# A preactivated convolution: sums and differences gathered in one PSUM bank, and two thirds of the images combined

## The chip, the cores and the metric

The kernel runs on one core of a Trainium2 chip. The metric is device time in microseconds, the median of the runs. The engines are named as in the profile: PE is TensorE, PEld its weight loads, DVE is VectorE, ACT is ScalarE, POOL is GpSimd, SP is SyncE, which here issues DMAs only.

## The reference

The input `x` is 160 images of 128 channels and 32 x 32 pixels. Each is normalised over groups of 4 channels, convolved 3 x 3 (padding 1) with one of 5 weight sets (image b*5+n in the reshaped batch uses set n), and added to `x`. The weights are quantised first, by two nested floors.

```python
    # weights: w = s1*floor(U/s1) + s2*floor((U - v1)/s2), s1 = (max U - min U)/3, s2 = s1/5
    w = (v1 + v2).reshape(OUT_CH * N, IN_CH, K, K)
    xb = x.reshape(B // N, N * C, H, W)
    act = conv_general_dilated(xb, w, window_strides=(1, 1), padding=[(1, 1), (1, 1)], feature_group_count=N)
    ...
    # _gn: 32 groups of 4 channels, over channels and pixels
    ((g - m) / jnp.sqrt(s + 1e-5)).reshape(v.shape)
    ...
    x = x + _L0_conv_ref(_gn(x), L0_conv_U)
```

## The kernel before

**Tiling.** One image is one step: 128 channels on the partitions, 1024 pixels along them. The kernel's own index i runs over the images of one weight set after the other, 32 per set. Images come in chunks of two (`load`, L492) and go out twice: `store_input` writes the input itself to the output, and `accumulate` (L949) later adds the convolution to it in DRAM with an accumulating DMA issued by GpSimd. Only the first three and the last four images (`by_hand`) are added by VectorE.

**Fewer multiplications.** Two neighbouring outputs of a 3-tap filter (g0, g1, g2) are made of four products instead of six: with inputs d0 to d3, the products are (d0-d2)g0, (d1+d2)(g0+g1+g2)/2, (d2-d1)(g0-g1+g2)/2 and (d1-d3)g2. Even is the sum of the first three, odd is the second minus the third minus the fourth. In the code the four are quarters 0, 2, 3 and 1 of a tile of 2048 columns. The weights of quarters 2 and 3 are called SUM and DIFF and are made by `both_sums` (L571).

**Two kinds of images.** Values are in float16, as a high part and a low part (what rounding left over).

- A *combined* image (`combined`, L651) takes the four combinations of neighbouring columns in float32 (`combine` on VectorE, L684; `beside_pairs` on GpSimd, L701), then the high part vh (`high_combined`, ScalarE, L735) and the low part vl (`low_combined`, VectorE, L741). Both go through four quarters of three matmuls: 24 matmuls.
- An image that is *not combined* is normalised to z (GpSimd, or ScalarE for some), its high part goes through all nine taps for each parity of rows (`taps`, L775: 18 matmuls), and only its low part through the four quarters (`combinations`, L758: 12 matmuls): 30 matmuls.

From image 7 to 29 every second image is combined, from 30 to 129 three of five, then three of four.

**One round.** The loop in `run` (L983) goes over i. TensorE does in `conv(i)` (L862): the quarters 3 and 2 of image i+1, as `sums_of_pairs` (L854), into the banks m2 and m1a or m1b; then `main(i, 0)` and `main(i, 1)` (L878), which add quarters 0 and 1 (and the taps) on top of the even and the odd bank of image i. In the same round ScalarE copies half of m2 to SBUF (`leave`, L888), and VectorE writes both banks of image i+1 with two instructions:

```python
        nc.vector.scalar_tensor_tensor(even, m1, 0.5, m2, ALU.mult, ALU.add)
        between()
        nc.vector.scalar_tensor_tensor(odd, m1, 0.5, m2, ALU.mult, ALU.subtract)
```

The PSUM holds two pairs of banks (`eo`, four banks), m1a, m1b, m2 and one bank for small things. The finished pair of banks of image i-1 is copied to SBUF by ScalarE (`residual`, L921, one copy of 1024 columns) for the accumulating DMA.

**Order.** It is written out by hand: each engine runs its instructions in the order of the code. In a round ScalarE does the first measurement pass of an image some 15 ahead, `residual(i-1)`, `leave(i+1)`, a high part, the second measurement pass. VectorE does a low part with its combinations, steps of the next weight set's quantisation (`later`), `pairs(i+1)`, `combine`, and, for a few images (`BY_VECTOR`), the whole measurement. `step_of` (L973) tells which image a step is for; from round 11 on the three preparing steps run one image further ahead than before, so that rounds 11 to 13 each hold one step more.

Of the kernel before, what the change touches and what calls it, by code (L numbers as in the profile page):

```python
# [25 lines left out]

LIFT = 2.0**14
LEAST, MOST = 2.0**-10, 0.04
# [357 lines left out]
class Main:  # L386
# [41 lines left out]
    def __init__(self, tc, ctx, keep, x, u, out):  # L428
        self.tc = tc
        nc = self.nc = tc.nc  # L430
        self.imgs, C, self.H, self.W = x.shape
        P = self.P = nc.NUM_PARTITIONS
        assert C == P and self.H * self.W == 1024
        self.per_set = self.imgs // N_SETS
        self.xv = x.rearrange("(b n) c h w -> n c b (h w)", n=N_SETS)
        self.ov = out.rearrange("(b n) c h w -> n c b (h w)", n=N_SETS)
        self.uv = u.rearrange("n (o i k) -> n o i k", o=C, k=TAPS)

        def pool(name, bufs, **kw):
# [12 lines left out]
        self.evac = pool("evac", 2)  # L452
        self.sums = pool("sums", 3)
        self.unread = pool("unread", 1)
        self.small = pool("small", 3)
        self.ps_eo = pool("ps_eo", 2, space=PSUM)
        ps_m = pool("ps_m", 1, space=PSUM)
        ps_small = pool("ps_small", 1, space=PSUM)
        self.steps = Steps(nc, keep)

        self.m1a, self.m1b, self.m2_ps = (
            ps_m.tile([P, self.H // 2, self.W], F32, tag=name, name=name)
            for name in ("m1a", "m1b", "m2")
        )
        self.pair = [self.m1a, self.m2_ps]
# [3 lines left out]
        self.chunks, self.z, self.hi, self.v, self.eo, self.m2 = {}, {}, {}, {}, {}, {}  # L469
        self.sum, self.stored = {}, {}  # L470
        self.tables, self.wts, self.across = {}, {}, {}
        self.columns = []
# [48 lines left out]
    def over_partitions(self, ext1, ident, between):  # L521
# [3 lines left out]

        place = self.bank_pair("range").rearrange("p h r w -> p h (r w)")
        rows = place[0:1, 0, : 2 * P].rearrange("p (k c) -> p k c", k=2)
        for k in range(2):
# [3 lines left out]
        nc.vector.tensor_reduce(top, rows, AX.X, ALU.max)  # L532
        spread = place[:, 1, :2]
        nc.tensor.matmul(spread, self.ones, top, start=True, stop=True)
# [71 lines left out]
    def by_vector(self, i):  # L606
        return i in self.BY_VECTOR

# [42 lines left out]
    def combined(self, i):  # L651
# [123 lines left out]
    def taps(self, i, part, col, target, parities=(0, 1)):  # L775
# [7 lines left out]
        for k in self.KS:  # L783
            for a in parities:
# [3 lines left out]
                nc.tensor.matmul(  # L788
                    self.bank(target, a)[:, first:end, c0:c1],
                    self.wts[n, col][:, k, :],  # L790
# [5 lines left out]

    def bank_pair(self, i):
        return self.ps_eo.tile([self.P, 2, self.H // 2, self.W], F32, tag="eo", name=f"eo{i}")

    def bank(self, target, h):  # L800
        return target[h] if isinstance(target, list) else target[:, h]

    def warm_up(self, count):


        zeros = self.los[3].rearrange("p h w -> p (h w)")
        for _ in range(count):
            self.nc.tensor.matmul(
                self.pair[0].rearrange("p i w -> p (i w)"), zeros[:, :128],
                zeros[:, :512], start=True, stop=True,  # L810
            )

    def direct_hi(self, i, col):

        if i not in self.eo:
            self.eo[i] = self.bank_pair(i) if i < 2 else self.pair
        self.taps(i, (self.hi[i], 0), col, self.eo[i])
# [28 lines left out]

    def m1(self, i):
        return self.m1b if i % 2 else self.m1a
# [12 lines left out]

    def conv(self, i, on_the_way):  # L862


        if self.FIRST < i < self.imgs - 1:
            self.sums_of_pairs(i + 1)
        if i == self.FIRST:
            self.main(i, 0)
            self.sums_of_pairs(i + 1)
            on_the_way(self.COLS[1])  # L870
            self.main(i, 1)
            on_the_way(self.COLS[2])
        else:
            self.main(i, 0, lambda: on_the_way(self.COLS[1]))
            self.main(i, 1, lambda: on_the_way(self.COLS[2]))
        del self.v[i]

    def main(self, i, a, between=lambda: None):  # L878

        to = self.bank(self.eo[i], a)  # L880
        for step in self.KS:
# [6 lines left out]
    def leave(self, i):  # L888

        m2 = self.evac.tile([self.P, self.H // 2, self.W], F32, tag="m2", name=f"m2_{i}")  # L890
        self.nc.scalar.mul(m2, self.m2_ps, 0.5)  # L891
        self.m2[i] = m2

    def pairs(self, i, between=lambda: None):


        nc = self.nc
        m1, m2 = self.m1(i), self.m2.pop(i)
        eo = self.eo[i] = self.bank_pair(i)
        if i == self.imgs - 1:  # L900
            eo = self.eo[i] = [eo[:, 0], self.m1(i - 1)]
        even, odd = (self.bank(eo, a) for a in range(2))
        nc.vector.scalar_tensor_tensor(even, m1, 0.5, m2, ALU.mult, ALU.add)
        between()
        nc.vector.scalar_tensor_tensor(odd, m1, 0.5, m2, ALU.mult, ALU.subtract)  # L905

# [5 lines left out]

    def flat(self, i, banks):
        return banks.rearrange("p a i w -> p a (i w)") if self.combined(i) else banks

# [5 lines left out]
    def residual(self, i):  # L921
# [19 lines left out]
        image = self.as_banks(i, xj)  # L941
        if eo is self.pair:
            for a in range(2):
                nc.vector.tensor_add(image[:, a], self.bank(eo, a), image[:, a])
        else:
            nc.vector.tensor_add(image, self.flat(i, eo), image)
        self.store(i)
# [35 lines left out]
    def run(self):  # L983
# [42 lines left out]
        for i in range(2):  # L1026
            self.measure(i)
        first_means = self.bank_pair("means").rearrange("p h r w -> p h (r w)")
        spread = self.over_partitions(
            ext1, ident, lambda: self.stats_of(0).means(first_means[:, 0])  # L1030
        )
# [32 lines left out]
        measure(1, 3)  # L1064
        self.stats[1].means(first_means[:, 1])
        self.stats[1].deviations()
# [48 lines left out]
        for i in range(self.imgs):  # L1115
# [15 lines left out]
            if i < self.FIRST:  # L1131
                if i == self.FIRST - 1:
                    self.sums_of_pairs(self.FIRST)

                j = (i - 1) % self.FIRST
                self.direct_hi(j, self.COLS[2])
                self.direct_lo(j, self.COLS[2])
                if i == 0:
                    self.stats[2].variances()
# [26 lines left out]
            if i < self.FIRST:  # L1166
# [6 lines left out]
                if i == 2:  # L1173
                    self.leave(3)
                    self.normalise(5)
                    measure(1, 9)
                    self.high_part(5)
                    self.pairs(3)
                    self.low_part(4)
# [3 lines left out]
            else:  # L1183
# [132 lines left out]
```

## Time and profile before

| | |
|---|---|
| median of 3 runs | 966.45 us (965.62 to 966.77) |
| profiled execution | 964.56 us, span 962.5 us |
| granted TensorE clock | 0.995 |
| PE busy | 927.8 us (96%), 4432 matmuls |
| DVE busy | 902.6 us (94%) |
| ACT busy | 862.7 us (90%) |
| POOL busy | 460.1 us (48%) |
| DMA | 254.22 MB, mean 264 GB/s |

The page gives the busy time of each engine, its share in 40 slices of the span, and groups of instructions with the number, the mean duration, and what ended the idle time before them. In its names, `m` is m2 (the PSUM bank and its copy alike, since numbers are left out), `eo` the pairs of banks, `vh` and `vl` the high and low parts of a combined image, `hi`, `lo` and `rows` those of the others. A matmul's duration (0.37 us) holds a part that overlaps the next one; the distance from start to start (0.21 us) is what it takes of TensorE.

### The profile page before, as it was taken

What the parts mean: (1) busy time and instruction counts of PE and PEld (TensorE: products, weight loads), DVE (VectorE), ACT (ScalarE), POOL (GpSimd) and SP (SyncE); (2) the same over time, 40 slices, a digit from 0 to 9 for tenths busy, and PEclk for the clock granted to TensorE, in tenths of its full rate; (3) what the DMA queues carried; (4) which work ended last, traced back from release to release, by engine and by line L of the source; (5) the groups of instructions that cost most, each with busy time, mean ns of one, the idle gap of its engine ahead of it and who ended that gap; (6) DMA issues with size and microseconds to landing.
All of it is one profiled execution on the core that took longest, in us unless ns stands there. A gap on an engine that the chain in (4) does not pass through costs nothing.

```text
span 962.5 us, 13034 instructions
## 1 busy us (share of the span) xinstructions
PE 927.8 (96%) x4432; PEld 433.8 (45%) x4432; DVE 902.6 (94%) x1269; ACT 862.7 (90%) x1167; POOL 460.1 (48%) x477
## 2 busy tenths in 40 slices
PE   2899989999999999999999999999999999999997
PEld 1344434444444444444444444444444444444443
DVE  7989999999899999989999999899999998999993
ACT  5879989999899999999999999999999999997660
POOL 4344434456445445554545445545444366565640
PEclk9999999999999999999999999999999999999999
DMA  9079999999999999999999999999999999856563
GB/s 349 36 267 345 334 348 320 325 321 325 328 321 323 317 295 308 272 306 254 295 251 289 284 293 297 282 277 286 267 273 267 282 279 269 172 91 107 91 107 112
DMA packets 67450, 254.22 MB, mean 264 GB/s; under 512 B 5296, under 2 KB 5296, under 8 KB 67376
## 3 DMA queue, kind: packets, MB, share of 16 engines
q1 hardware_dynamic: 45344, 173.09, 48.0%
q0 software_dynamic: 22032, 80.23, 44.4%
q8 instruction: 36, 0.59, 0.2%
q14 instruction: 38, 0.31, 0.1%
HBM read 89.19 MB, written 164.10 MB: 263 GB/s over the span
## 4 chain that ended last, share of the span: by engine, by line


## 5 line engine op out<-in xcount | busy, mean ns | idle before, releaser
L788 PE MATMUL eo<-hi,wt 128*128 128x496 f16 (+3 forms) x1170 | 310.8, 376 | 2.4 <-DVE eo L905 1.7
L843 PEld LDWEIGHTS <-wt 128*128 128x128 f16 x1884 | 183.9, 99 | 211.5 <-DVE eo L905 2.7
L744 DVE SCALAR_TENSOR_TENSOR vl<-v,rstd,vh 128x2048 f16<-128x2048 f32 x94 | 221.8, 2360 | 0.2 <-ACT vh L738 0.2
L843 PE MATMUL eo<-vh,wt 128*128 128x512 f16 x561 | 210.1, 375 | 1.2 <-DVE eo L905 1.2
L843 PE MATMUL eo<-vl,wt 128*128 128x512 f16 x561 | 210.1, 374 | 0.0
L738 ACT ACTIVATE vh<-v,rstd 128x2048 f16<-128x2048 f32 x94 | 188.2, 2002 | 4.8 <-DVE v L697 4.3
L929 ACT COPY sum<-eo 128x1024 f32<-128x1024 f32 x153 | 161.0, 1052 | 32.3 <-PE eo L843 31.7
L788 PEld LDWEIGHTS <-wt 128*128 128x128 f16 x1242 | 121.2, 99 | 142.8 <-DVE eo L905 4.9
L678 POOL TENSOR_SCALAR v<-xt,ngm 128x64 f32<-128x64 f32 x94 | 79.1, 842 | 202.0 <-DVE vl L744 86.9
L248 ACT ACTIVATE junk<-xt,mv 128x1024 uint8<-128x1024 f32 x152 | 174.4, 1148 | 0.3
L241 ACT ACTIVATE junk<-xt 128x1024 uint8<-128x1024 f32 x152 | 160.5, 1056 | 13.3 <-DMA xt<-in_x_dram 10.0
L714 POOL TENSOR_SCALAR z<-xt,ngm,rstd 128x1024 f32<-128x1024 f32 x49 | 93.3, 1904 | 165.1 <-DVE rows L773 55.0
L843 PEld LDWEIGHTS <-across 128*128 128x128 f16 x1128 | 110.8, 98 | 131.9 <-issue 4.9
L843 PE MATMUL eo<-rows,wt 128*128 128x512 f16 x378 | 143.5, 380 | 0.0
L953 POOL DMA_DIRECT2D out_dram<-sum x153 | 133.7, 874 | 14.4 <-ACT sum L929 6.6
L690 DVE TENSOR_TENSOR v<-xt 128x960 f32<-128x960 f32 x94 | 114.0, 1212 | 0.0
L843 PE MATMUL m<-vl,across 128*128 128x496 f16 (+1 forms) x282 | 106.4, 377 | 2.1 <-DVE vl L744 2.1
L891 ACT ACTIVATE m<-m 128x512 f32<-128x512 f32 x157 | 93.7, 597 | 14.1 <-PE m L843 13.7
L843 PE MATMUL m<-vh,across 128*128 128x496 f16 (+1 forms) x282 | 106.2, 376 | 0.2 <-ACT m L891 0.2
L708 POOL TENSOR_TENSOR v<-xt 128x512 f32<-128x512 f32 x94 | 97.2, 1034 | 0.0
L751 DVE TENSOR_TENSOR lo<-z,hi 128x1024 f16<-128x1024 f32 x66 | 80.6, 1221 | 0.0
L286 POOL TENSOR_TENSOR rstd<-ve,mhalf 128x8 f32<-128x8 f32 (+2 forms) x24 | 42.3, 1761 | 65.1 <-DVE rows L773 21.1
(150 smaller groups left out, 1166.3 us busy)
## 6 DMA issues: line engine op xcount, KB each, us to landing
xt<-in_x_dram SPq DMA_DIRECT2D x78, 1024.0 KB, 9.6
out_dram<-sum POOLq DMA_DIRECT2D x153, 512.0 KB, 8.7
out_dram<-xt SPq DMA_DIRECT2D x76, 1024.0 KB, 14.2
out_dram<-xt SPq DMA_DIRECT2D x7, 512.0 KB, 3.3
u<-in_L_conv_U_dram SPq DMA_DIRECT2D x4, 576.0 KB, 13.6
xt<-in_x_dram SPq DMA_DIRECT2D x4, 512.0 KB, 10.1
range<-in_L_conv_U_dram SPq DMA_DIRECT2D x3, 576.0 KB, 8.3
u<-in_L_conv_U_dram SPq DMA_DIRECT2D x2, 288.0 KB, 3.1
```

The source lines that it names most:

```text
L241: self.nc.scalar.activation(junk, image, ACTF.Copy, scale=-1.0 / image.shape[1], accum_out=self.mv[:, j, 0:1],)
L248: self.nc.scalar.activation(junk, image, ACTF.Square, bias=self.mv[:, j, 0:1], accum_out=self.mv[:, j, 1:2],)
L690: nc.vector.tensor_tensor(self.view(v, 1, (511, 2), (half, H), (1, half - 1)), self.view(x, 1, (1, 2), (W, H), (2, half - 1)), self.view(x ...
L708: ins = nc.gpsimd.tensor_sub(self.v[i][:, 1536:], odd, even)
L714: ins = nc.gpsimd.tensor_scalar(z, self.image(i), st.ngm[:, j], st.rstd[:, j], ALU.add, ALU.mult)
L738: self.nc.scalar.mul(vh, self.v[i], st.rstd[:, j])
L744: yield self.nc.vector.scalar_tensor_tensor(vl, self.v[i], st.rstd[:, j], self.hi[i], ALU.mult, ALU.subtract)
L788: nc.tensor.matmul(self.bank(target, a)[:, first:end, c0:c1], self.wts[n, col][:, k, :], tile[:, s0 : s0 + 2 * (end - first) - 1 : 2, c0 + ...
L843: self.nc.tensor.matmul(out, weights, moving, start=start and j == 0, stop=False, skip_group_check=True)
L891: self.nc.scalar.mul(m2, self.m2_ps, 0.5)
L929: nc.scalar.copy(self.as_banks(i, self.sum[i]), self.flat(i, eo))
L953: added = self.nc.gpsimd.dma_start(self.ov[n, :, b], self.sum.pop(i), accum_op=ALU.add)
```

## The change

- *The banks.* PSUM is now four banks for even, three for odd, one small. The sums (quarter 2) go straight into the even bank of their image (`begin`). ScalarE copies that bank (`leave`). Then the differences (quarter 3) are added in the same bank (`complete`), which then holds sum + difference. VectorE makes the odd bank alone, as twice the copy minus the even bank (`odd_from_even`). The factor of one half goes into the weights (`both_sums` has one more multiplication), and LIFT, which scales weights against activations, is halved.
- *The order.* In rounds 3 to 13 `begin(i+1)`, `leave(i+1)` and `complete(i+1)` lie in one round, around `main(i, 0)`. From round 15 on `conv(i)` runs `complete(i+1)`, `begin(i+2)`, `main(i, 0)`, `main(i, 1)`, and `leave(i+2)` takes the place of `leave(i+1)` in ScalarE's order.
- *The copies.* `residual` copies the two banks one by one, since they are no longer neighbours.
- *The images.* From 30 to 129 two of three are combined, in place of three of five. Every eighth image above 32 is measured by VectorE, in place of ScalarE.

```diff
-LIFT = 2.0**14
+LIFT = 2.0**13
...
-        self.ps_eo = pool("ps_eo", 2, space=PSUM)
-        ps_m = pool("ps_m", 1, space=PSUM)
+        self.ps_even = pool("ps_even", 4, space=PSUM)
+        self.ps_odd = pool("ps_odd", 3, space=PSUM)
...
         yield engine.tensor_tensor(total, g0, g2, ALU.add)
+        yield engine.tensor_tensor(total, total, g1, ALU.add)
+        yield engine.tensor_scalar_mul(total, total, 0.5)
         yield engine.tensor_tensor(diff, total, g1, ALU.subtract)
-        yield engine.tensor_tensor(total, total, g1, ALU.add)
...
     def by_vector(self, i):
-        return i in self.BY_VECTOR
+        return i in self.BY_VECTOR or i > 32 and i % 8 == 0
...
-        return i % 5 % 2 == 0 if i < self.THIRDS else i % 4 != 2
+        return i * 2 % 3 < 2 if i < self.THIRDS else i % 4 != 2
...
-    def sums_of_pairs(self, i):
-
-        for quarter, kind, target in (
-            (3, self.DIFF, self.m2_ps), (2, self.SUM, self.m1(i))
-        ):
-            for step in self.KS:
-                self.product(target, i, quarter, step, kind, start=step == self.KS[0])
+    def begin(self, i):
+
+        even = self.bank_of(self.ps_even, i)
+        self.eo[i] = [even]
+        for step in self.KS:
+            self.product(even, i, 2, step, self.SUM, start=step == self.KS[0])
+
+    def complete(self, i):
+
+        for step in self.KS:
+            self.product(self.eo[i][0], i, 3, step, self.DIFF)
+
+    def steady(self, i):
+
+        return i > self.FURTHER + 2
 
     def conv(self, i, on_the_way):
 
-        if self.FIRST < i < self.imgs - 1:
-            self.sums_of_pairs(i + 1)
-        if i == self.FIRST:
+        ahead = range(i + 1, self.imgs)[:1]
+        if self.steady(i) and self.steady(i - 1):
+            for k in ahead:
+                self.complete(k)
+            for k in range(i + 2, self.imgs)[:1]:
+                self.begin(k)
+            self.main(i, 0, lambda: on_the_way(self.COLS[1]))
+            self.main(i, 1, lambda: on_the_way(self.COLS[2]))
+        elif i == self.FIRST:
             self.main(i, 0)
-            self.sums_of_pairs(i + 1)
+            self.begin(i + 1)
             on_the_way(self.COLS[1])
             self.main(i, 1)
             on_the_way(self.COLS[2])
+            self.leave(i + 1)
+            self.complete(i + 1)
         else:
+            self.begin(i + 1)
             self.main(i, 0, lambda: on_the_way(self.COLS[1]))
+            self.leave(i + 1)
+            self.complete(i + 1)
+            if self.steady(i):
+                self.begin(i + 2)
             self.main(i, 1, lambda: on_the_way(self.COLS[2]))
...
     def leave(self, i):
 
-        m2 = self.evac.tile([self.P, self.H // 2, self.W], F32, tag="m2", name=f"m2_{i}")
-        self.nc.scalar.mul(m2, self.m2_ps, 0.5)
-        self.m2[i] = m2
-
-    def pairs(self, i, between=lambda: None):
-...
-        nc.vector.scalar_tensor_tensor(even, m1, 0.5, m2, ALU.mult, ALU.add)
-        between()
-        nc.vector.scalar_tensor_tensor(odd, m1, 0.5, m2, ALU.mult, ALU.subtract)
+        half = self.half[i] = self.evac.tile(
+            [self.P, self.H // 2, self.W], F32, tag="half", name=f"half{i}"
+        )
+        self.nc.scalar.copy(half, self.eo[i][0])
+
+    def odd_from_even(self, i):
+
+
+        even, odd = self.eo[i][0], self.bank_of(self.ps_odd, i)
+        self.eo[i].append(odd)
+        self.nc.vector.scalar_tensor_tensor(
+            odd, self.half.pop(i), 2.0, even, ALU.mult, ALU.subtract
+        )
...
-            nc.scalar.copy(self.as_banks(i, self.sum[i]), self.flat(i, eo))
+            image = self.as_banks(i, self.sum[i])
+            for a in range(2):
+                nc.scalar.copy(image[:, a], self.flat(i, eo[a]))
...
-                if i + 1 < self.imgs:
-                    self.leave(i + 1)
+                if self.steady(i) and i + 2 < self.imgs:
+                    self.leave(i + 2)
...
                 if i + 1 < self.imgs:
-                    self.pairs(i + 1)
+                    self.odd_from_even(i + 1)
```

More of the change, by code (lines that the diff above doesn't have):

```diff
@@ L455, in __init__ @@
         self.small = pool("small", 3)
-        self.ps_eo = pool("ps_eo", 2, space=PSUM)
-        ps_m = pool("ps_m", 1, space=PSUM)
+        self.ps_even = pool("ps_even", 4, space=PSUM)
+        self.ps_odd = pool("ps_odd", 3, space=PSUM)
         ps_small = pool("ps_small", 1, space=PSUM)
         self.steps = Steps(nc, keep)
[L461 to L465, printed above, removed]
         small = ps_small.tile([P, 512], F32, tag="small", name="small")
         self.pt, self.pg = small[:, : ROW * P].rearrange("p (k o) -> p k o", k=ROW), small[:, ROW * P :]
-        self.chunks, self.z, self.hi, self.v, self.eo, self.m2 = {}, {}, {}, {}, {}, {}
+        self.chunks, self.z, self.hi, self.v, self.eo, self.half = {}, {}, {}, {}, {}, {}
         self.sum, self.stored = {}, {}
         self.tables, self.wts, self.across = {}, {}, {}
-        self.columns = []
+        self.columns, self.warm = [], None
         cuts = [0, 2, 4, 8, 12, 16, 20, *range(24, self.imgs + 1, 8)]
@@ L524, in over_partitions @@
         nc, P = self.nc, self.P
-        place = self.bank_pair("range").rearrange("p h r w -> p h (r w)")
-        rows = place[0:1, 0, : 2 * P].rearrange("p (k c) -> p k c", k=2)
+        place = [self.bank_of(pool, "range").rearrange("p r w -> p (r w)") for pool in (self.ps_even, self.ps_odd)]
+        rows = place[0][0:1, : 2 * P].rearrange("p (k c) -> p k c", k=2)
         for k in range(2):
@@ L532, in over_partitions @@
         nc.vector.tensor_reduce(top, rows, AX.X, ALU.max)
-        spread = place[:, 1, :2]
+        spread = place[1][:, :2]
         nc.tensor.matmul(spread, self.ones, top, start=True, stop=True)
@@ L788, in taps @@
                 nc.tensor.matmul(
-                    self.bank(target, a)[:, first:end, c0:c1],
+                    target[a][:, first:end, c0:c1],
                     self.wts[n, col][:, k, :],
@@ L795, in taps, with bank_of @@
                 )
[L797 to L801, printed above, removed]
+    def bank_of(self, pool, name):
+        tag = "even" if pool is self.ps_even else "odd"
+        return pool.tile([self.P, self.H // 2, self.W], F32, tag=tag, name=f"{tag}{name}")
     def warm_up(self, count):
         zeros = self.los[3].rearrange("p h w -> p (h w)")
+        if self.warm is None:
+            self.warm = self.bank_of(self.ps_odd, "warm")
         for _ in range(count):
             self.nc.tensor.matmul(
-                self.pair[0].rearrange("p i w -> p (i w)"), zeros[:, :128],
+                self.warm.rearrange("p i w -> p (i w)"), zeros[:, :128],
                 zeros[:, :512], start=True, stop=True,
@@ L815, in direct_hi @@
         if i not in self.eo:
-            self.eo[i] = self.bank_pair(i) if i < 2 else self.pair
+            self.eo[i] = [self.bank_of(pool, i) for pool in (self.ps_even, self.ps_odd)]
         self.taps(i, (self.hi[i], 0), col, self.eo[i])
@@ L845, in product @@
             )
-    def m1(self, i):
-        return self.m1b if i % 2 else self.m1a
     def both(self, i):
         return ([self.hi[i]] if self.combined(i) else []) + [self.v[i]]
-    def sums_of_pairs(self, i):
-        for quarter, kind, target in (
-            (3, self.DIFF, self.m2_ps), (2, self.SUM, self.m1(i))
-        ):
-            for step in self.KS:
-                self.product(target, i, quarter, step, kind, start=step == self.KS[0])
-    def conv(self, i, on_the_way):
-        if self.FIRST < i < self.imgs - 1:
-            self.sums_of_pairs(i + 1)
-        if i == self.FIRST:
+    def begin(self, i):
[8 more added lines that the diff above has]
+        return i > self.FURTHER + 2
+    def conv(self, i, on_the_way):
+        ahead = range(i + 1, self.imgs)[:1]
[7 more added lines that the diff above has]
+        elif i == self.FIRST:
             self.main(i, 0)
-            self.sums_of_pairs(i + 1)
+            self.begin(i + 1)
             on_the_way(self.COLS[1])
@@ L878, in main @@
     def main(self, i, a, between=lambda: None):
-        to = self.bank(self.eo[i], a)
+        to = self.eo[i][a]
         for step in self.KS:
@@ L888, in leave @@
     def leave(self, i):
-        m2 = self.evac.tile([self.P, self.H // 2, self.W], F32, tag="m2", name=f"m2_{i}")
-        self.nc.scalar.mul(m2, self.m2_ps, 0.5)
-        self.m2[i] = m2
-    def pairs(self, i, between=lambda: None):
[L897 to L902, printed above, removed]
-        nc.vector.scalar_tensor_tensor(even, m1, 0.5, m2, ALU.mult, ALU.add)
-        between()
-        nc.vector.scalar_tensor_tensor(odd, m1, 0.5, m2, ALU.mult, ALU.subtract)
+        half = self.half[i] = self.evac.tile(
[8 more added lines that the diff above has]
+        )
     def as_banks(self, i, image):
@@ L911, in as_banks, with flat @@
         return image.rearrange("p (i a w) -> p a i w", a=2, w=self.W)
-    def flat(self, i, banks):
-        return banks.rearrange("p a i w -> p a (i w)") if self.combined(i) else banks
+    def flat(self, i, bank):
+        return bank.rearrange("p i w -> p (i w)") if self.combined(i) else bank
     def by_hand(self, i):
@@ L941, in residual @@
         image = self.as_banks(i, xj)
[L942 to L946, printed above, removed]
+        for a in range(2):
+            nc.vector.tensor_add(image[:, a], self.flat(i, eo[a]), image[:, a])
         self.store(i)
@@ L1027, in run @@
             self.measure(i)
-        first_means = self.bank_pair("means").rearrange("p h r w -> p h (r w)")
+        first_means = [self.bank_of(pool, "means").rearrange("p r w -> p (r w)") for pool in (self.ps_even, self.ps_odd)]
         spread = self.over_partitions(
-            ext1, ident, lambda: self.stats_of(0).means(first_means[:, 0])
+            ext1, ident, lambda: self.stats_of(0).means(first_means[0])
         )
@@ L1064, in run @@
         measure(1, 3)
-        self.stats[1].means(first_means[:, 1])
+        self.stats[1].means(first_means[1])
         self.stats[1].deviations()
@@ L1132, in run @@
                 if i == self.FIRST - 1:
-                    self.sums_of_pairs(self.FIRST)
+                    self.begin(self.FIRST)
+                    self.leave(self.FIRST)
                 j = (i - 1) % self.FIRST
@@ L1137, in run @@
                 self.direct_lo(j, self.COLS[2])
+                if i == self.FIRST - 1:
+                    self.complete(self.FIRST)
                 if i == 0:
@@ L1173, in run @@
                 if i == 2:
-                    self.leave(3)
                     self.normalise(5)
@@ L1177, in run @@
                     self.high_part(5)
-                    self.pairs(3)
+                    self.odd_from_even(3)
                     self.low_part(4)
```

## The prediction

> **What bounds the kernel now.** I read the page's busy times and slices first, then the windows, the waits of TensorE, and the order of time inside two images. From the page:
>
> ```profile
> PE 927.8 (96%) x4432; PEld 433.8 (45%) x4432; DVE 902.6 (94%) x1269; ACT 862.7 (90%) x1167; POOL 460.1 (48%) x477
> PE   2899989999999999999999999999999999999997
> PEclk9999999999999999999999999999999999999999
> ```
>
> Three engines are above 90%, so the shares do not decide. The windows do (columns: busy us and instruction count of PE, PEld, DVE, ACT, POOL, then clock and DMA):
>
> ```profile
> 125.00:130.00 5.00, 2.73 (x14) 1.12 (x12) 4.90 (x13) 5.00 (x6) 0.00 (x0) 0.97 1.04 349
> 130.00:135.00 5.00, 4.30 (x13) 1.47 (x12) 4.97 (x9) 3.71 (x8) 2.05 (x2) 0.69 1.03 378
> 350.00:800.00 450.00, 449.04 (x2156) 210.41 (x2155) 431.63 (x595) 433.69 (x591) 224.44 (x214) 1.00 1.01 282
> ```
>
> From 350 to 800 us TensorE is busy 449 of 450 us at full clock; VectorE and ScalarE have 4% to spare. The exception is 125 to 135 us, where TensorE stands still while VectorE is full. TensorE's waits there:
>
> ```profile
> PE m L843 <- DVE vl L744: 2.1, 1, 2.1
> PE eo L788 <- DVE eo L905: 1.7, 2, 1.0
> PE m L843 <- ACT m L891: 0.2, 1, 0.2
> ```
>
> So: TensorE bounds images 15 to 159, and VectorE bounds a short stretch where the order of work is pulled forward by one image (rounds 11 to 14). A busy TensorE need not be one at its peak, so I took the price of an image from the order of time (start, duration):
>
> ```profile
> 505.79 0.38 PE L843 MATMUL m<-vh,across 128*128 128x512 f16 x1
> 508.32 0.38 PE L843 MATMUL eo<-vh,wt 128*128 128x512 f16 x1
> 510.86 0.81 PE L843 MATMUL m<-rows,wt 128*128 128x512 f16 x3
> ```
>
> A combined image takes 2.53 us for sums and differences and 2.54 us for its main part, 5.07 us for 24 matmuls. For an image that is not combined, the main part ran from 500.68 to 505.79 (5.11 us, 24 matmuls), and its sums and differences from 87.81 to 89.11 in an earlier round (1.30 us, 6 matmuls): 6.41 us. Every matmul starts 0.21 us after the one before; nothing is left between them.
>
> DMA reads as busy all the time (1.01), but moves 282 GB/s there against 346 at 60 to 125 us, and no engine waits for an image to be loaded after 60 us. I take it as not binding.
>
> [...] after 2.1 us without work, matmuls started 0.41 us apart. [...] In the trace a 1024-column copy lasts 1.05 us, but the next starts 0.89 to 0.97 us after it; a 512-column one lasts 0.60 and is followed after 0.49.
>
> **The change, part by part.**
>
> *More combined images.* From 30 to 130 the rule took 3 of 5 (60 images); 2 of 3 are 67. Seven images go from 6.41 to 5.07 us: 7 x 1.34 = 9.4 us less on TensorE, 42 matmuls. That is on the path that sets the end. Each costs ScalarE 0.95 us (high part: 1.90 between starts against 0.95) and VectorE about 1.5 us (2.36 + 1.21 + 0.74 against 1.22 + 0.69 + 0.42 + 0.42, less overlap); GpSimd's 0.84 + 1.03 against 1.90 is even.
>
> *Sums and differences in the even bank.* TensorE's counts stay. VectorE loses one 0.69 us instruction per image (0.72 between starts; 157 images, 113 us in all). ScalarE's `leave` stays one 512-column read from PSUM, 0.60. Beside TensorE's saturated stretch the loss on VectorE is worth nothing, since VectorE had 4% to spare; it matters where VectorE was late, below.
>
> *Two evacuating copies.* 153 times one 1024-column copy becomes two of 512: +0.01 to +0.09 us by starts, +0.14 if nothing overlapped. I take 0.08: 12 us on ScalarE, hidden while it has time.
>
> *Every eighth image measured by VectorE.* Images 40, 48, ... 152, 15 of them: ScalarE loses two passes with their accumulator reads (1.15 + 1.05 between starts, 2.2 us), VectorE gains 1.7 (125.80 to 127.48 in the trace). Per image ScalarE stands at 433.69/450 x 5.60 = 5.40 us (5.60 being TensorE's mean at 60% combined); + 0.08 + 0.07 - 0.28 gives 5.27 of a new period of 5.51 (two thirds at 5.07, one at 6.41). VectorE stands at 5.37 - 0.72 + 0.21 + 0.10 = 4.96. Both stay under TensorE with more room than before, so the 9.4 us should come through whole.
>
> *Steady rounds (i > 14).* TensorE's order is now differences of i+1, sums of i+2, main of i. `leave(i+2)` stands behind `residual(i-1)` on ScalarE and can start 2.6 us into the round; it ends at 3.2 and is due at the next round's start, 5.07: 1.9 us spare. Behind it stand the high part and the second measurement, both rounds ahead of need. The sums use vl one round earlier than before, but VectorE makes it ahead of `odd_from_even(i)`, for which the main part waits anyway: no new wait. The even bank of i+2 needs image i-2 copied, which ScalarE does a round before. Cost 0; if ScalarE is over 1.9 us late, the rest shows on TensorE.
>
> *Rounds 3 to 13.* Here `leave(i+1)` comes first in ScalarE's round, and `complete(i+1)` on TensorE waits for it inside the same round: a new wait in a tight place, with the second main half queued behind it, and `odd_from_even(i+1)` behind that. Gain first: VectorE saves 0.72 x 11 = 7.9 us ahead of the stretch in which its vl came 2.4 us late. So these go: 2.3 us at 127 to 130, six matmuls at half clock (6 x 0.2 = 1.2), 0.7 at 134, 1.0 at 158, 0.8 at 66: 6.0 us. Against it: in round 9 ScalarE would wait for TensorE's sums from 97.3 to 100.1 instead of 1.2 us for the residual, so it is 1.7 us later from there on. In round 10 it started at 105.8; `leave(11)` then ends at 108.1, where TensorE wants to go on at 107.2: 0.9. In round 13 it started at 124.8; with 1.7 and the split copies, `leave` ends at 127.6 where TensorE, itself 0.9 later, is ready at 125.8: 1.8. The first hand-over (rounds 3 and 4, differences, then VectorE, then main with only 0.65 us of other work between) costs about 0.5. Sum 3.2. Net gain 2.8, bounds 6 and -2 (each of 11 rounds losing 0.7).
>
> *Small.* One more multiplication per sum of weights: on GpSimd 3 x 0.45 and 0.9 us at the start (it idles from 57.8 to 66.7; at most 0.4 us on the path through the third column), on VectorE 8 x 0.35 us in all, in its spare time. LIFT only rescales. The tail keeps its two adds and last stores: 0.
>
> Sum: 9.4 + 2.8 = 12.2 us, against the profiled execution's own 964.56 us (span 962.5): 952.4. The median of the runs is 1.9 us above that execution, so I state 954.5.
>
> **The rivals.** A measurement of this kernel tells 0.2% (1.9 us) from no change.
>
> 1. *Matmuls alone*: the new wait of rounds 3 to 13 eats all that VectorE gives back. For it: ScalarE is 100% busy from 105 to 130 us. 966.45 - 9.4 = 957.0. Chance 0.20.
> 2. *All early stalls go*: ScalarE finds its phase and the hand-overs are hidden. 966.45 - 9.4 - 6.0 = 951.0. Chance 0.10.
> 3. *ScalarE becomes the bound*, the slower side: in each steady round it waits first for the main part (residual), then for the sums (leave), and cannot use the time, since its queue is in order. It has 5.51 - 5.27 = 0.24 us per image to give; from 0.33 us lost per image it is slower than the 5.60 of before. At 0.5 us: 5.77 against 5.60, 0.17 x 130 images = 22 us, 988. Against it: if it falls behind by 1 us both waits are over when it arrives, and 1.9 us are spare. Chance 0.06.
> 4. *The cover of matmuls is not what it seems*: DMA, at 1.01, is what holds the pace; then the change in images brings nothing and only noise is left: 964 to 968. Against it: no wait on an image. Chance 0.04.
>
> The likeliest (0.60) is the sum above, 954.5, with 952 to 957 as its own range. The range 950.5 to 961 takes in rivals 1 and 2 and the bound of -2 for rounds 3 to 13 (966.45 - 9.4 + 2 = 959), with some ScalarE waiting in the steady rounds. Faster 0.90, same 0.04, slower 0.06.
>
> **What would show it.** Right: 42 fewer f16 matmuls; TensorE still full from 200 to 900 us; the stand at 125 to 135 us gone or smaller, its wait named on ScalarE's copy instead of vl; VectorE near 90% in the middle, waiting for TensorE before L903's successor; ScalarE at 95 to 96%. Wrong: TensorE idle on ScalarE's copy in steady rounds, or ACT without idle time from 350 to 800 us; a longer start before 70 us; matmuls in the even bank further apart than 0.21 us.

## The result, and the profile after

The changed kernel takes 973.89 us (median of 4 runs, 973.39 to 975.66) against 966.61 for the kernel before in the same comparison: a ratio of 1.0079, 95% interval 1.0063 to 1.0095. It is slower by 7.3 us, where 954.5 was forecast. The profiled execution took 974.27 us (span 972.5).

The line of busy times on the page of the changed kernel:

```profile
PE 922.3 (95%) x4390; PEld 430.3 (44%) x4390; DVE 900.9 (93%) x1192; ACT 840.5 (86%) x1259; POOL 463.9 (48%) x489
```

TensorE has the 42 matmuls less that were announced. VectorE has 77 instructions less and is as busy as before, 900.9 us against 902.6. That is the surprise: 157 instructions of 0.69 us left it, 108 us in all, and only some 36 us of work were to be added (15 x 1.7 and 7 x 1.5). The windows of the changed kernel (busy us and count of PE, PEld, DVE, ACT, POOL, then clock and DMA):

```profile
130.00:135.00 5.00, 2.13 (x10) 0.79 (x9) 4.96 (x8) 4.68 (x7) 0.00 (x0) 0.99 1.04 332
135.00:140.00 5.00, 3.37 (x9) 1.18 (x9) 4.44 (x6) 1.52 (x4) 2.84 (x3) 0.50 1.02 420
350.00:800.00 450.00, 441.06 (x2107) 205.52 (x2106) 437.55 (x556) 418.80 (x630) 224.56 (x219) 1.00 1.00 278
```

In the middle TensorE was full for all but 1 us; now it stands for 9 of 450 us, and VectorE is the fullest engine. The stop near 130 us is longer than before, and so is the stretch at a granted clock of 0.50: 135 to 141 us here, 130 to 133 us in the kernel before. The longest of TensorE's waits on VectorE and ScalarE, and ScalarE's on TensorE (us in total, times, longest):

```profile
ACT half L906 <- PE even L838: 54.6, 42, 7.3
...
PE even L838 <- DVE vl L739: 10.3, 12, 1.7
...
PE even L838 <- ACT half L906: 5.7, 8, 1.8
PE even L783 <- DVE odd L913: 3.8, 3, 2.8
```

In the steady rounds TensorE waits above all for VectorE's low part (between 160 and 900 us 8.6 us, against 2.4 us for ScalarE's copy), in the early ones for ScalarE's copy and for VectorE's odd bank (between 60 and 160 us 3.3 and 3.0 us). ScalarE waits 55 us for TensorE's sums, but it has that time: it is not what TensorE waits for longest.

Where the time went, from the start of the even main part of an image in the two traces (worked out by counting matmuls in the order of the code; us from the span's start):

| image | before | after | difference |
|---|---|---|---|
| 10 | 105.9 | 104.9 | -1.0 |
| 15 | 141.0 | 148.1 | +7.1 |
| 30 | 228.5 | 234.5 | +6.0 |
| 130 | 795.9 | 804.3 | +8.4 |
| 159 | 953.1 | 961.8 | +8.7 |

Two losses, then: 8 us between images 10 and 15, and between 30 and 130 a stretch that should have become 9.4 us shorter and became 2.4 us longer, 12 us off. The size of the first is uncertain: two variants of the kernel before that have the same instructions up to image 15 reach it at 142.8 and 144.4 us, so up to 3.4 us of the 8 may be chance.

**The row that explains the second loss.** The same instruction, `combine`'s subtraction of columns on VectorE (128 x 960, both inputs in SBUF), in the groups of the kernel before and then of the changed one (busy us, mean ns):

```profile
L690 DVE TENSOR_TENSOR v<-xt 128x960 f32<-128x960 f32 x94 | 114.0, 1212 | 0.0
```

```profile
L685 DVE TENSOR_TENSOR v<-xt 128x960 f32<-128x960 f32 x101 | 177.5, 1758 | 1.6 <-POOL v L673 1.6
```

0.55 us more each time, with nothing changed in it. In the order of time of the kernel before, VectorE and GpSimd beside each other:

```profile
508.60 0.70 DVE L903 SCALAR_TENSOR_TENSOR eo<-m1a,m 128x512 f32<-128x512 f32 x1 [0.17 <-PE m1a L843]
508.65 1.03 POOL L708 TENSOR_TENSOR v<-xt 128x512 f32<-128x512 f32 x1
509.34 0.70 DVE L905 SCALAR_TENSOR_TENSOR eo<-m1a,m 128x512 f32<-128x512 f32 x1
...
509.94 1.15 DVE L690 TENSOR_TENSOR v<-xt 128x960 f32<-128x960 f32 x1
```

and of the changed kernel:

```profile
561.03 0.68 DVE L913 SCALAR_TENSOR_TENSOR odd<-half,even 128x512 f32<-128x512 f32 x1
561.32 1.03 POOL L703 TENSOR_TENSOR v<-xt 128x512 f32<-128x512 f32 x1
561.63 1.76 DVE L685 TENSOR_TENSOR v<-xt 128x960 f32<-128x960 f32 x1
```

Before, GpSimd's subtraction (1.03 us) ran beside two VectorE instructions of 0.70 us that read PSUM and only one operand from SBUF. With one of them gone, VectorE is at its next instruction, with two SBUF operands, while GpSimd is still at work. Over all combined images GpSimd's subtraction overlaps L690 by 0.08 us in the mean before and L685 by 0.73 us after, and a straight line through the 101 durations gives 1.13 us plus 0.87 us for each us of overlap: VectorE stands almost still in the overlap. Why L685 grows in the overlap is not shown by the traces; they show the overlap and the lengths. The name of the helper, `beside_pairs`, said where GpSimd's work was meant to go.

### The profile page after: what moved, and what is told of

Its sections match the earlier page's. It is cut to its first block, busy times and chain, and to the rows that moved or that the text cites. A ratio compares the mean times of both kernels' runs of the same rounds, so it can differ in the third digit from the quotient of the medians.

```text
span 972.5 us, 12946 instructions
## 1 busy us (share of the span) xinstructions
PE 922.3 (95%) x4390; PEld 430.3 (44%) x4390; DVE 900.9 (93%) x1192; ACT 840.5 (86%) x1259; POOL 463.9 (48%) x489
## 4 chain that ended last, share of the span: by engine, by line
DVE 49%; PE 32%; ACT 8%; issue 6%; POOL 4%; DMA 0%; POOLq 0%; DVEq 0%; ACTq 0%
PE even L838 17%; DVE vl L739 12%; DVE v L685 10%; PE odd L838 5%; PE even L783 5%; PE odd L783 4%; DVE odd L913 4%; DVE v L692 4%; DVE lo L746 4%; POOL rstd L286 3%; ACT vh L733 2%; ACT junk L248 2%; DVE st L231 2%; ACT junk L241 1%; DVE rows L759 1%
## 5 line engine op out<-in xcount | busy, mean ns | idle before, releaser
L838 PE MATMUL even<-vl,across 128*128 128x496 f16 (+1 forms) x606 | 226.9, 374 | 10.4 <-DVE vl L739 10.3
L838 PE MATMUL even<-vh,across 128*128 128x496 f16 (+1 forms) x606 | 227.1, 375 | 4.4 <-ACT half L906 4.3
L685 DVE TENSOR_TENSOR v<-xt 128x960 f32<-128x960 f32 x101 | 177.5, 1758 | 1.6 <-POOL v L673 1.6
L783 PEld LDWEIGHTS <-wt 128*128 128x128 f16 x1116 | 109.3, 100 | 130.2 <-issue 6.8
L838 PE MATMUL even<-rows,wt 128*128 128x496 f16 (+1 forms) x504 | 155.0, 381 | 1.6 <-ACT half L906 1.5
L783 PE MATMUL even<-hi,wt 128*128 128x512 f16 (+1 forms) x531 | 146.2, 379 | 4.8 <-DVE odd L913 3.8
L906 ACT COPY half<-even 128x512 f32<-128x512 f32 x157 | 92.9, 592 | 61.8 <-PE even L838 54.6
L783 PE MATMUL odd<-hi,wt 128*128 128x512 f16 (+1 forms) x531 | 144.3, 375 | 0.0
L913 DVE SCALAR_TENSOR_TENSOR odd<-half,even 128x512 f32<-128x512 f32 x157 | 107.6, 686 | 11.7 <-PE even L838 9.2
L838 PE MATMUL even<-vh,wt 128*128 128x496 f16 (+1 forms) x303 | 113.5, 375 | 0.1
L838 PE MATMUL odd<-vl,wt 128*128 128x496 f16 (+1 forms) x303 | 113.5, 375 | 0.0
L838 PE MATMUL even<-vl,wt 128*128 128x496 f16 (+1 forms) x303 | 113.5, 374 | 0.0
L838 PE MATMUL odd<-vh,wt 128*128 128x496 f16 (+1 forms) x303 | 113.4, 374 | 0.0
```

Source lines behind the costliest of these rows:

```text
L685: nc.vector.tensor_tensor(self.view(v, 1, (511, 2), (half, H), (1, half - 1)), self.view(x, 1, (1, 2), (W, H), (2, half - 1)), self.view(x ...
L783: nc.tensor.matmul(target[a][:, first:end, c0:c1], self.wts[n, col][:, k, :], tile[:, s0 : s0 + 2 * (end - first) - 1 : 2, c0 + dw : c1 + dw],
L838: self.nc.tensor.matmul(out, weights, moving, start=start and j == 0, stop=False, skip_group_check=True)
L906: self.nc.scalar.copy(half, self.eo[i][0])
L913: self.nc.vector.scalar_tensor_tensor(odd, self.half.pop(i), 2.0, even, ALU.mult, ALU.subtract)
```

## The experiments

Theories. *Lost cover*: VectorE pays the collision above, and its load paces the steady rounds. *Plain load*: VectorE is late because of the added measurements and combined images, whatever GpSimd does. *Early hand-over*: the loss before image 15 comes from ScalarE's copy lying between sums and differences in one round.

**GpSimd writes zeros.** The collision is taken away, not the instruction; the fourth quarter of the combined images is left out of the result.

```diff
-            ins = nc.gpsimd.tensor_sub(self.v[i][:, 1536:], odd, even)
+            ins = nc.gpsimd.memset(self.v[i][:, 1536:], 0.0)
```

> The changed kernel with one thing altered: GpSimd's subtraction odd - even of a combined image (L703, reads SBUF, 1.04 us) is a memset of zeros in the same place, which reads nothing; so the fourth quarter of combined images is left out of the result. Theory of the lost cover (GpSimd's subtraction used to run beside two VectorE instructions that read PSUM; with one left it runs into VectorE's L685, which has two inputs in SBUF): L685 falls from 1.76 to about 1.2 us, VectorE's busy time by 50 to 60 us, TensorE's idle time between 250 and 900 us from 11 us to under 4, and the time from 974 to 963-967. Theory of the plain load (VectorE is late because of 15 measurements and 7 more combined images, whatever GpSimd does): L685 stays near 1.7 us and the time at 972-975.

Measured: 963.86 us (ratio to the kernel before 0.9968, 95% interval 0.9955 to 0.998; the same two figures stand in brackets below), 10.0 us under the changed kernel. Two lines of it, the group and a window:

```profile
L685 DVE TENSOR_TENSOR v<-xt 128x960 f32<-128x960 f32 x101 | 116.9, 1157 | 1.6 <-POOL v L673 1.6
```

```profile
350.00:800.00 450.00, 448.31 (x2153) 210.29 (x2152) 410.77 (x571) 424.34 (x642) 195.43 (x223) 1.00 1.02 284
```

L685 is back at 1.16 us, VectorE's busy time falls by 65 us to 835.7, and TensorE is full again. The forecast of the lost cover holds. A memset is also shorter than a subtraction (0.58 against 1.04 us) and reads nothing; the next runs get at the same thing with all work in place.

**The odd bank twice.** The second instruction of the pair is put back as idle work, where a combination follows.

```diff
-        self.nc.vector.scalar_tensor_tensor(
-            odd, self.half.pop(i), 2.0, even, ALU.mult, ALU.subtract
-        )
+        half = self.half.pop(i)
+        nxt = self.step_of(i - 1, 4)
+        for _ in range(1 + any(self.combined(k) for k in nxt)):
+            self.nc.vector.scalar_tensor_tensor(odd, half, 2.0, even, ALU.mult, ALU.subtract)
```

> The changed kernel, in which VectorE makes the odd bank twice over (same instruction, same operands) in each round in which it afterwards combines an image: 101 more instructions of 0.69 us, 70 us of work added to an engine that is busy 97% of the middle. Theory of the lost cover: the second one covers GpSimd's subtraction again as the old pair did, L685 falls back to 1.15-1.3 us, the two effects cancel, and the time stays at 971-977. Theory of the plain load: VectorE gets 0.47 us more per image in the mean than the 5.5 us it hardly meets, and the time goes to 1010 or more.

Measured: 982.00 us (1.016, 1.0143 to 1.0176). 101 added instructions, 70 us by their durations, raise VectorE's busy time by only 19 us, since L685 gives back 49:

```profile
L685 DVE TENSOR_TENSOR v<-xt 128x960 f32<-128x960 f32 x101 | 128.5, 1272 | 0.9 <-POOL v L673 0.8
```

The cover works (1.27 us; an overlap under 0.05 us in 80 of 101), and the plain load's 1010 us is out. But the two effects do not cancel, though I had expected them to: 0.49 us come back for 0.69 spent, and 8 us are lost.

**GpSimd later, in the kernel before.** No instruction is added or moved in VectorE's order; only GpSimd's subtraction for the image that is being combined (`beside`, which `beside_pairs` now returns) is made to wait for the second instruction of the pair.

```diff
...
-                    self.pairs(i + 1)
+                    second = self.pairs(i + 1)
+                    for ins in beside:
+                        if ins is not None:
+                            self.after(ins, second.ins)
```

> The kernel before, in which only GpSimd's subtraction of a combined image (L708) is released later: when VectorE has ended the second instruction of the pair (the odd bank), not an instruction ahead of the pair. No instruction is added, none leaves VectorE's order. Theory of the lost cover: L690 now meets GpSimd's subtraction every time and goes from 1.21 to 1.7-1.8 us, 94 x 0.55 = 52 us more on VectorE; at 5.4 us per image of TensorE's 5.6 VectorE is then over the pace by about 0.1 us, and the time rises from 967 to 976-990. If the collision is only a companion of the loss: L690 may lengthen but the time stays within 2 us of 967.

Measured: 1006.56 us (1.0407, 1.0382 to 1.0431), 40 us slower than the kernel before. The three groups beside each other:

```profile
L709 POOL TENSOR_TENSOR v<-xt 128x512 f32<-128x512 f32 x94 | 165.2, 1757 | 98.0 <-DVE eo L907 97.7
L697 DVE SCALAR_TENSOR_TENSOR v<-xt,twice 128x512 f32<-128x512 f32 x94 | 133.5, 1421 | 0.0
L690 DVE TENSOR_TENSOR v<-xt 128x960 f32<-128x960 f32 x94 | 117.3, 1248 | 0.0
```

The collision alone, in the old kernel, costs far more than the whole change. It fell on other rows than I expected: L690 takes 1.25 us in the mean, GpSimd's subtraction 1.76 against 1.03, and L697, VectorE's next one, 1.42 against 0.74. From these means I estimate that L690 was mostly the first of the two; in the round at 510 us it was not (GpSimd at 510.27, L690 at 510.33), and there L690 took 1.99 us and GpSimd 1.03. VectorE has 64 us more to do, at 98.4% busy from image 30 to 130, and it has not the slack that I gave it, which is why 976 to 990 was too low.

**Only one rule of the change, on the kernel before.** `combined` takes two of three.

```diff
-        return i % 5 % 2 == 0 if i < self.THIRDS else i % 4 != 2
+        return i * 2 % 3 < 2 if i < self.THIRDS else i % 4 != 2
```

> The kernel before with one part of the change alone: two of three images combined from 30 to 129. TensorE has 42 matmuls less, 7 x 1.34 = 9.4 us. VectorE gets 0.10 us more per image (5.47 of a new period of 5.51) and ScalarE 0.07 (5.47). Theory of the prediction (the pace from 30 on is TensorE's, and the cover of the two instructions is in place): 957-960. If VectorE at 5.47 of 5.51 is in fact the pace already: 963-967, with TensorE waiting for vl or for the second instruction of the pair.

Measured: 966.40 us against 966.64 (0.9994, 0.9985 to 1.0003): nothing, where TensorE has 9.4 us less to do.

```profile
350.00:800.00 450.00, 442.78 (x2118) 205.62 (x2116) 441.56 (x588) 436.25 (x588) 228.65 (x221) 1.00 1.00 281
```

VectorE is at 98.1%, and TensorE waits for the second instruction of the pair, between 160 and 900 us:

```profile
PE eo L843 <- DVE eo L905: 8.0, 10, 1.6
```

The kernel before was already as near to VectorE's limit as to TensorE's.

**Both rules on images, on the kernel before.**

```diff
-        return i in self.BY_VECTOR
+        return i in self.BY_VECTOR or i > 32 and i % 8 == 0
```

> The kernel before with both parts of the change that do not concern the banks: two of three images combined, and every eighth image above 32 measured by VectorE. VectorE is then at 5.37 + 0.10 + 0.21 = 5.68 us per image, over TensorE's 5.51. Theory that VectorE's load is what decides: it sets the pace, 0.17 x 115 = about 20 us over the 957 of TensorE: 972-980, with TensorE waiting for vl. If VectorE's load is not what decides: 957-960.

Measured: 985.67 us (1.0194, 1.0176 to 1.0213). Without the new banks the two rules cost 19 us; VectorE's load decides, and costs 6 to 14 us more than the 972 to 980 expected. TensorE's wait is again for the second instruction of the pair (21.4 us between 160 and 900 us), not for vl.

**The changed kernel without the eighth image.** The line above taken back.

> The changed kernel without the rule for every eighth image: ScalarE measures images 40, 48, ... 152 again. VectorE loses 15 x 1.7 = 25 us, ScalarE gets 33 to 38 us back. If VectorE's total load sets the pace from 30 to 150 (both theories on VectorE say that the load counts): TensorE's waits on vl go, 966-969. If ScalarE's copy of the even bank is what is short (my prediction's third rival): ScalarE is over 5.5 us per image, and the time rises to 978 or more.

Measured: 964.54 us (0.9979, 0.997 to 0.9987), 9.4 us under the changed kernel and faster than the kernel before. That is better than the 966 to 969 expected. Taking the 15 measurements from VectorE is enough (its busy time falls by 29 us), and TensorE's waits on vl are gone. ScalarE, at 98.8% between images 30 and 130, still does not set the pace: TensorE waits 4.3 us for its copy between 160 and 900 us, but with zeros by GpSimd it waits 3.4 us with ScalarE at 94.4%, so ScalarE's load makes little of this wait.

**The early rounds in the old way.** Images 5 to 15 have their differences (quarter 3) in the odd bank at once, ScalarE's copy in its old place, and two instructions on VectorE.

```diff
         else:
             self.begin(i + 1)
+            self.differences(i + 1)
             self.main(i, 0, lambda: on_the_way(self.COLS[1]))
-            self.leave(i + 1)
-            self.complete(i + 1)
...
+            self.nc.vector.scalar_tensor_tensor(odd, half, -1.0, even, ALU.mult, ALU.add)
+            self.nc.vector.scalar_tensor_tensor(even, half, 1.0, even, ALU.mult, ALU.add)
```

> The changed kernel, in which images 5 to 15 are made in the old way (sums in the even bank, differences in the odd one, both at the start of the round before, ScalarE's copy in its old place, two VectorE instructions); all later ones as in the change. Theory of the early hand-over (in rounds 4 to 14 TensorE waits in the same round for ScalarE's copy, and ScalarE for TensorE's sums): the 7 us that the change loses between the main parts of images 10 and 15 (5 to 6 us if VectorE's old stop at 128 us comes back) go, time 967-970. If the early loss comes from the second copy of the residual or from VectorE's longer L685 instead: within 2 us of 974.

Measured: 971.03 us (1.0045, 1.0028 to 1.0061), 2.9 us under the changed kernel: a gain, but less than forecast. Image 15's main part starts at 145.9 us, between 148.1 (changed) and 141.0 (before). The order of time of the changed kernel shows the hand-over; TensorE first, then ScalarE:

```profile
109.41 0.38 PE L838 MATMUL even<-vh,across 128*128 128x512 f16 x1 [1.82 <-ACT half L906]
...
128.49 0.81 PE L838 MATMUL even<-rows,wt 128*128 128x512 f16 x3 [1.27 <-ACT half L906]
...
132.62 0.38 PE L838 MATMUL even<-vl,across 128*128 128x512 f16 x1 [1.70 <-DVE vl L739]
...
136.63 1.41 PE L783 MATMUL even<-hi,wt 128*128 128x512 f16 x3 [2.80 <-DVE odd L913]
```

```profile
100.48 0.59 ACT L906 COPY half<-even 128x512 f32<-128x512 f32 x1 [2.54 <-PE even L838]
```

The first two waits are gone in this experiment; the stop at 132 to 137 us, on VectorE, stays (2.42 and 2.13 us). Part of what remains is not a property of the code: the kernel before and its two variants with other rules on images have the same instructions up to here, and image 15 starts at 141.0, 142.8 and 144.4 us in their traces.

**Both single edits together.**

> The changed kernel with the early rounds in the old way and without the rule for every eighth image, the two single edits together. If their gains (2.9 and 9.4 us) lie in different stretches, as the main parts' start times say, they add: 961-963. If each only shortened the same lateness of VectorE: 964-965.

Measured: 960.21 us (0.9925, 0.9903 to 0.9947), 13.7 us under the changed kernel, and 6.4 under the kernel before: the best of all runs. 2.9 and 9.4 add, and a little more, so that the time is just under the 961 to 963 expected.

**Only the banks, the order and the two copies.** The changed kernel without both rules on images.

> The changed kernel without both rules on images: three of five combined as before, no eighth image measured by VectorE; only the banks, the order and the two copies are changed. From the runs so far VectorE would need 5.17 us per image from 30 to 130 and ScalarE 5.46, both under TensorE's 5.67. Theory that VectorE's load and the early rounds are all there is to the loss: main parts from 30 to 130 at 5.67 us as before, the early loss stays (5 to 7 us by image 15), time 971-974. If the new order of sums and differences costs TensorE something in every round: 976 or more.

Measured: 970.79 us (1.0046, 1.0031 to 1.0061): 4.2 us slower than before, just under the 971 to 974 expected, and all of it lost before image 30: in the traces image 30 starts 7.1 us later than in the kernel before, image 159 6.4 us later. From 30 to 130 it needs 5.66 us per image, as the kernel before. The steady order costs TensorE nothing, and the relief of VectorE is worth nothing as long as no work is put in its place.

**Every sixteenth image by VectorE, with the early rounds in the old way.**

> The version with the early rounds in the old way, with every sixteenth image (48, 64, ... 144) measured by VectorE, in place of every eighth or none. ScalarE, 5.53 us per image and 99% busy without any, goes to about 5.40; VectorE from 5.31 to about 5.42 of 5.58. Theory that both engines now fit under TensorE: the last 4 us of TensorE's waits on ScalarE's copy between 160 and 900 us go, 957-960. If VectorE at 5.42 is already too near the pace: 961-965.

Measured: 963.43 us (0.9968, 0.9959 to 0.9977): a miss, 3.2 us above the version without any. VectorE and ScalarE are both at 96%, as was meant, but TensorE's waits on ScalarE's copy and on vl did not go (3.9 and 1.6 us between 160 and 900 us). What makes the waits on the copy, if not ScalarE's load, was not taken apart.

**The steady rounds in one table**, from the traces between the main parts of images 30 and 130. TensorE's own price is taken as the 5.67 us of the kernel before at three of five, and as 9.4/100 less, 5.58, at two of three. Not in the table are the versions with only the early rounds altered (5.70 us with the eighth image, 5.60 without), which here have the code of "changed" and "changed, no eighth".

| kernel | us per image | VectorE busy, us | ScalarE busy, us |
|---|---|---|---|
| before | 5.67 | 5.45 (96.0%) | 5.48 (96.5%) |
| banks alone | 5.66 | 5.15 (91.1%) | 5.49 (97.0%) |
| zeros by GpSimd | 5.59 | 5.10 (91.2%) | 5.28 (94.4%) |
| changed, no eighth | 5.60 | 5.31 (94.9%) | 5.53 (98.8%) |
| early two, sixteenth | 5.62 | 5.41 (96.3%) | 5.41 (96.2%) |
| changed | 5.70 | 5.53 (97.0%) | 5.30 (93.1%) |
| before, rule | 5.67 | 5.56 (98.0%) | 5.51 (97.1%) |
| odd bank twice | 5.78 | 5.65 (97.8%) | 5.31 (91.9%) |
| before, both rules | 5.85 | 5.76 (98.5%) | 5.27 (90.1%) |
| before, GpSimd late | 5.96 | 5.87 (98.4%) | 5.49 (92.0%) |

VectorE begins to show at 5.41 us and paces from about 5.5 on: in the last five rows the time per image is VectorE's busy time and 0.09 to 0.17 us more. ScalarE at 98.8% does not pace.

## Why the prediction was wrong

**The step that failed** is in the part on every eighth image: "VectorE stands at 5.37 - 0.72 + 0.21 + 0.10 = 4.96." It measured 5.53, and 5.70 us per image were needed where 5.51 were forecast. The term that is missing from this sum is what happens to VectorE's next instruction when the second of the pair no longer stands between it and GpSimd; it was put at nothing. Of the 0.57 us, 0.37 are L685's 0.55 us in two of three images, 0.07 the longer vl (2.46 against 2.36 us; in 19 of the 23 that took over 2.45 us, GpSimd's normalising of another image was already at work when it began), and 0.08 the starting point: I turned a busy share into time with 5.60 us per image, which left out stalls and small matmuls; the trace between images 30 and 130 gives 5.67 and 5.45. 0.05 us is left over. The zeros and the late GpSimd show the collision as cause, in both kernels; the removed instruction took 0.72 us, but its removal brought back 0.55 of it in each combined image. I had costed its removal as a pure gain and named no work that it hid, on the engine beside it.

**The sum.** 12.2 us were to be gained and 7.3 were lost, 19.5 us apart. The banks and the order alone lost 4.2 us where 2.8 were to be gained: 7.0. The two rules on images, put on top of them, lost 3.1 us where 9.4 were to be gained: 12.5. Of the signs that were named for a right prediction only the 42 matmuls came: from 350 to 800 us VectorE was at 97% and not near 90%, ScalarE at 93% and not 95 to 96%.

**"VectorE had 4% to spare"** was read as slack. The rule alone on the kernel before shows what it was worth: 0.1 us more per image took all of TensorE's 9.4 us. From image 30 to 130 VectorE, which must follow TensorE round by round, set the pace in these runs at 97 to 98.5% busy.

**The matmuls** went as forecast: 42 fewer, and from 30 to 130 the versions at two of three with VectorE at 95% or below need 5.59 to 5.60 us per image, 7.6 to 8.0 us less in all than before. The sum's 9.4 us was right in mechanism, somewhat high in size.

**Rounds 3 to 13.** The losses were forecast with their places: 0.9 us in round 10 and 1.8 in round 13, measured 1.82 and 1.27; ScalarE's idle 2.5 us in round 9 is there. The gain was not: "VectorE saves 0.72 x 11 = 7.9 us ahead of the stretch" assumed that it could run ahead. It waited instead, for the differences of the round and for vh (7.5 and 1.9 us between 60 and 160 us): from 80 to 150 us it was busy 69.0 us before and 59.1 after, so the time saved became idle time, and the vl of image 15 started at 130.2 us, before at 127.5. So the early part lost about 4 us (banks alone: 4.2), where a gain of 2.8 was forecast. The second copy, taken as 0.08 us per image, was dearer in the sum than in the trace: ScalarE needs 5.49 us per image with the banks alone and 5.48 before. That undoing the hand-over brings 2.9 to 4.3 us (with and without the eighth image) is shown; how the rest of the stop at image 15 divides between the split copies, the granted clock of 0.50 and chance from run to run is open, and was not taken apart.

**Rivals.** The one on the slower side had the right sign and the wrong engine: ScalarE waits in its order, as described (54.6 us), but of the three engines it is the one that could afford it. The slower case that happened, VectorE at the pace, had no place among the four.

**The eighth image** was a trade in the wrong direction: it put 1.7 us on the engine that was short of time, and took 2.2 us off one that was not; that cost 9.4 us in the end.

## What to carry to other kernels

When an instruction is removed, ask what ran beside it on the other engines, and what will run beside that in its place (here L685 went from 1.21 to 1.76 us): look at the neighbour's rows in the order of time, not only at the engine's sum. A busy share of 96% on an engine that follows another round by round need not be a reserve (here it was none): test it by adding 0.1 us per round before counting on it. When two parts of a change trade load between engines, run each alone: here one line taken back, and the early order kept, turn a loss of 7.3 us into a gain of 6.4.

## What the runs showed of the hardware

- With GpSimd's subtraction overlapping it by 0.73 us in the mean, L685 took 1.76 us; with 0.08 us, in the kernel before (L690), 1.21 us; with a memset on GpSimd in the same place, 1.157 us. In the run with GpSimd late L690 took 1.25 us in the mean, GpSimd's subtraction 1.76 (1.03 in the kernel before) and L697 1.42 (0.74).
- VectorE's instructions that make the even and odd banks, with one operand in PSUM and one in SBUF, kept their length beside GpSimd's subtraction (in the kernel before 0.70 us in the 94 with over 0.4 us of overlap and in the 161 with none).
- In the changed kernel TensorE stopped for 1.70 us ahead of 132.62 us and for 2.80 us ahead of 136.63 us. The granted clock was 0.99 from 130 to 135 us and 0.50 from 135 to 140, and the twelve matmuls from 136.63 us on took 5.0 us, against 2.6 at the 0.21 us from start to start of the steady rounds.
